# Four graph layers on one core: a new written order of steps, with buffers, first loads and both ends set anew

## The chip, the cores and the metric

The kernel runs on one NeuronCore of a Trainium2 chip. The metric is the device time of one execution in microseconds. Five engines work side by side, each through its own list of instructions in order: TensorE (PE, with weight loads shown as PEld), VectorE (DVE), ScalarE (ACT), GpSimd (POOL) and SyncE (SP), which here issues nearly all DMAs. A DMA that has to wait for its data holds up every DMA behind it in the same engine's queue.

## The reference, cut to what matters

There are 64 independent graphs, each with 256 nodes of 256 features (`x`) and a 256 x 256 adjacency (`adj`). Four layers follow each other, and each one adds its result to its input and normalizes the rows.

```python
x = layernorm(x + L0(x, adj))  # 4-head masked attention, output projection Wo, norm
x = layernorm(x + L1(x, adj))  # norm, 8-head masked attention on itself, MLP 256-1024-256 with gelu
x = layernorm(x + L2(x, adj))  # softmax of leaky_relu(s1_i + s2_j) over the mask, times x W
x = layernorm(x + L3(x, adj))  # softmax of leaky_relu(x diag(a_k) x^T) over the mask, times x
```

Everything is float32. For adjacencies of zeros and ones only, `L3` uses `a0` alone.

## The kernel before, in words

`usual_input` does all the work for adjacencies of zeros and ones that are the same both ways; a second path, `any_input`, follows for other inputs and isn't entered here. A flag that is worked out at the end decides.

One graph goes through seven Python generators, called threads, and every `yield` ends a step. A graph has 93 steps:

- `a` (19 steps, a0 to a18): a0 loads adj, a1 turns it to bf16 on ScalarE (`adjb`), a2 transposes it by DMA (`adjT`), a3 loads x twice, once as it is (`x0`) and once in blocks (`turned`). Then come the mask (VectorE), xT (a VectorE transpose of `turned`), x + beta, the projections q, k and v with their copies out of PSUM, the score products, two exponentials times mask, their sums `ea`, and the value product with the softmax sums.
- `u` (11): u0 inverts the sums on VectorE (`few`, `back`), u1 stores them to DRAM (`lines`), u2 loads them back spread over the partitions (`rr`), u3 multiplies; then the product with Wo, statistics, residual, norm (`z`, `xb`).
- `z` (4): stores z to DRAM (`rows`), loads it back in blocks (`blk`, four DMAs), turns the blocks on VectorE (`t`), scales them.
- `b` (8): second attention. `w` (9): its output goes through DRAM (w0 store, w1 load, w2 turn), statistics (w3), then the MLP's input does (w6 store, w7 load, w8 turn).
- `c` (8): first MLP product and gelu, four times. `o` (34): second MLP product, then layers 2 and 3; two more trips through DRAM, named n2 (o5 store, o6 load, o7 turn) and n3 (o18, o19, o20); o33 stores the result.

A transpose of a 256 x 256 tile is thus, in most places, a store of two DMAs, a load of four and one VectorE instruction. For the first and last graphs `DIRECT` names transposes that TensorE does instead; the first graph's x is one of them.

The order of all steps of all graphs is written out. `PLACES` gives each of the 93 steps a time in units of one graph's period; step i of graph g stands at g plus that time, and sorting gives one list. The list repeats with a period of 93 slots. `FIRST` and `LAST` are written lists of step names that replace its beginning (about the first seven graphs' worth) and its end (about nine). The wrapper `InOrder` keeps each engine's instructions in the order of this list; its line, 474, is therefore the line that nearly all instructions carry in the profile, so that they are told apart by their tiles. A wait comes from the data: an instruction waits until what it reads has been written, and until the last reader of the buffer that it writes is done. `BUFS` gives the number of buffers of each kind of tile.

`load_x(0)` and the loads of the first weights stand ahead of the list; further weights come in `l` steps on SP's queue, and `p` steps prepare constants.

Of the kernel before, what the change touches and what calls it, by code (L numbers as in the profile page):

```python
# [8 lines left out]
F32 = mybir.dt.float32  # L9
BF16 = mybir.dt.bfloat16  # L10
I32 = mybir.dt.int32
U8 = mybir.dt.uint8
AF = mybir.ActivationFunctionType
ALU = mybir.AluOpType
AX = mybir.AxisListType

P = 128
N = 256
D = 256
NC = D // P  # L20
G = 2
QB = N // P
# [19 lines left out]
SQ = True  # L42
XQ = True
DIRECT = {0: ('x', 'z', 'o'), 63: ('yT', 'n2', 'n3', 'o')}
BUFS = {'t': 5, 'q': 3, 'k': 2, 'v': 4, 'y': 4, 'z': 4, 'xb': 4, 'both': 3, 'xn': 6, 'mask': 8, 'e': 6, 'x0': 4, 'turned': 2, 'blk': 3, 'oT': 2, 'zs': 1, 'rr': 2, 'xT': 2, 'qT': 2, 'kT': 2, 'adj': 2, 'adjb': 2, 'adjT': 2, 'hT': 2}
PLACES = {
# [11 lines left out]
}  # L58
FIRST = (
    "a0a1l0a0a0a0a0a0a2a1a1a0a0a0a0a0a0a0a0a0a1a0a0a0a1a1a1a1a2a0u0a1a1l0a1p0a3a4a2u0a2a2a2a3a2a1a1a1a2u0u0u0a1a1"  # L60
    "a1u0a4a5a3l0a2a2a2u0a2a3l0a3a3u0u0a1a2a1u1a4a3a2a2a2a2u1u1a3a3a4a3a3a3a6u0u0a3a3u1a4a4a3a3a2a2z0a5z0a4a6l0l0"
    "u1u2l0a3u2u2z0z0a3p0u1u1a3u3u3u1a5b0b0a4u2b0b0p0u3a5b0u2u2b0a4a4a5u1a4a4a4u2u3a4a5u2a4l0a6u1z1a7a4u2b0b0u3u3"
    "w0w0a4a4w0a4u2z1z1u4a5a5w0u3a5a5z1p0a6a6u4a6a6p0w0u3a7p0z2z2z2u4a5w0u4a5a6a6a5a6a6w0w0u3b1b1b1b1b1b1w0u4u4z2"
    "b2b1c0p0u4u3z3z3b2b2b1b2c0c0b2z3w1w1u1a7w1c0c0c0c0c0w1o0w1b2o0o0o0z3b3b3b3u4b2a7w1b3b3b2b3a6w1a5a5a5a5w1w1w2"
    "o0o0w2a6a6b3a5b3a6o0a5a6u5u5c1c1c1c1c1a7c1c1a6a6w3a7c1u5a7a7u2w2w3o0u4a6a7u5u4w2w2z4u5u5w2u5a8a9u6u6z4u6o0w2"
    "u3w3u5z4o1o1u5w3w3w2a7u6z4b4o1o1o0o0o0a7b4w2u6b4b4u5b4o1u6w3z5a7a7w3z5b4w3c2c2z5o0z5a7o0o0o0o0u6c2c2c2c2c2u6"
    "c2o2o1o1o1o0o2u6o0o0u4a7a7b5a8a9b4o0o0o2a7a8a7b5b5w3b4a7b5o2o0b5b5u5o0o2a9w4u6w4w4w4w4o2o2c3c3c3c3c3c3c3c3o0"
    "o1o1z6b5o2b5o0o0o0o0o0o0z6z6o0o2a8a9o3o1o2o2u7o0z6w5o1o3aau7w4w4a8a8u7o3o3b6o2b6o1o1o1o1b6b6o3b6w5aau7b6w4o1"
    "w4a8a8a8a8a8a8o2o0o2o2o2a8a8o1a8a8w5c4c4o3a8w5c4c4c4o3c4c4c4o2u7u7u7o2o4w5o1o1o2o4o2o1o1w5aau7u7o1o1o4u7z7o3"
    "b6b6o2o2a8o4o1w6w5a8o1o1o1o1o1o1o1o2o2a9w5a9u8u8o3o3a9aba9w5a9a9a9a9a9a9o1o4u6o2o2u7o3w6o2w6w6o3o2o2c5a9a9c5"  # L70
    "u8u8abc5c5z7z7o3o3o3o3z7acc5a9aac5u8o4u8o4abo3o3o3o3c5c5u8o4a9aaaau8aab7aau8a9aaw6w6u9u9u9o4o4o3o2o2u8aao5o2"
    "b7b7z8b7o2aao4o4b7o5o1")
LAST = (
    "b7o5aaadw6o2o3o3u9o5aaw6u9z8o3aao5b7z8u9u9aaaaaao5z8b8o5u9o5b7b8b8aaaab8u9c6c6o4uao4c6o3c6o4o4c6w7w7w7o4u9c6"
    "c6c6o3o6o6uaz9w7w7w7uao3uaz9uaz9w7w7abo6o5b8b8uauaw7z9b9b9b8b9o5b8b9o5o5w8c7o4o4o4c7uao3o3uaabacababc7c7c7c7"
    "o5o5u8u9o6o3o3c7uac7abababo3w8w8abo4aco5o5acw8w8b9ababb9o3o7abzazao4o4o7o6w8o6w8ababo6abado5o7o4b9zazab9w9o7"
    "o7o4w8ababubo7o6acw9acbao4o4o4o4o5o4w8baado5aeo7o4o6o6acacacacbao4acacw9acbao5w9babaubo4ubo6o6w9c8c8c8afo5ub"
    "c8o7c8c8c8c8acacubaco3o4ubo6o6o5o5o5w9aco5adw9ado7o7adadacacucububaebabao7o7w9w9adadadadadadadubo5ucwao7ucuc"
    "o7o5o5adado6o5ubzbc9c9adafo7uco6o6o7uco7ucadado6o5o5o5o7c9udo8c9uawawawac9wac9zbududzbudzbucc9c9uco6o7ubbbo6"
    "o6bbo7o7o8o8uducududo8udzcbbzcaeo6wawabbo7o6o7o6o7o6o7zcbbaeo8udbbzco9o9o9udwawabco9bcbcbbbbaeaeaebczdzdbcbc"  # L80
    "cacacacacacacao5wbwbwbzdcawboaoaoaoazdbdbdwbbdbcbcbdo5afo6o7wbo6o6o7o8o8o6o7o7afafo9o6o6o7o7bdbdaeo6oawcwco7"
    "aeaeafafaeaeo6o9oawbwbbdbdo7o8ucwcaewcwco9oaaeaeaewbaewdwdo8o8wcwcudo9afafafafafafafafafaeafaeueueuewcoaafo8"
    "afo8o9oao9oawdwdcbcbo9oacbcbcbcbufueo9oawdo8o8ufo6o7o8wdo8o9o9oaoao9oao9oao8wco8wdo9ueueueueoacccccccccco9uf"
    "cbueccoaufwdcbwdo8o8o8ufufufufo8ueueobzeobufufzecczezezfcdcdobobo9ccbebebeo8o8oboazfzfo9ocoabebebeobococufzf"
    "cdo8bfbfbfcdbebebfcdcdocwecdcdo9oabfbfo8o8o9obobocododo8ododo8oao9weo9o8weodo8oaoaweobobocodo9oaocodbfbfo9oa"
    "o9oao9oaweweo9oaweocodweo9oao8o9oaobobo8ococodo9oaweobobobobodcecececececewfwfcecewfo8wfwfobocodo9o9obwfocod"
    "oeoeoeocococwfwfocoaoeoeobobodoaodododocwfcfcfodcfcfcfocoboboecfcfcfofofoeodoeoeocoeoeodofofofobocodococofoe"
    "odoeoeoeoeobofofodoeofofoboboboeobobofofobocobobofofofocofofobododoeoeococococococofofoeoeoeocofofofodododod"
    "odoeoeocofofododoeofoeoeoeoeoeodocofofoeofofofofofobocodoeodoeofof")
AHEAD = 16  # L90


# [356 lines left out]
def usual_input(ctx: ExitStack, tc: tile.TileContext, a: dict, out: bass.AP, flag: bass.AP):  # L449
# [62 lines left out]
    def load_edges(g):  # L512
        adj = new(io, [P, TB, N], I32, "adj")
        SP.dma_start(adj, a["adj"][g].rearrange("(q p) k -> p q k", p=P))
        return adj

    def load_x(g):
        turned = None
        if FX and "x" not in DIRECT.get(g, ()):
            turned = new(io, [P, NC, N // 32, 32], F32, "turned")  # L520
            parts = a["x"][g].rearrange("(t i) (c k j) -> k i c t j", i=32, c=NC, j=32)
            for k in range(P // 32):
                if XQ:
                    SP.dma_start(turned[32 * k:32 * k + 32], parts[k])
                for c in range(0 if XQ else NC):
                    SP.dma_start(turned[32 * k:32 * k + 32, c], parts[k, :, c])
        x0 = new(io, [P, TB, D], F32, "x0")
        SP.dma_start(x0, a["x"][g].rearrange("(q p) d -> p q d", p=P))
        return x0, turned
# [22 lines left out]
    def load_column(src, n, name, queue=None):  # L552

        t = const.tile([P, n // P], F32, name=name)
        load(queue, t, src.rearrange("(c p) -> p c", p=P))
        return t
# [3 lines left out]
    def load_all(src, name, at=None, queue=None):  # L560
# [2 lines left out]
        load(queue, t, src.unsqueeze(0).to_broadcast([P, D]))  # L563
        return t

    x_first = load_x(0)
    first = load_edges(0), x_first
    wqT = load_rows("L0_gnn_WqT", D, ACT)
    wkT = load_rows("L0_gnn_WkT", D, ACT)
    bq = load_column(a["L0_gnn_bq"], D, "bq", ACT)  # L570
    bk = load_column(a["L0_gnn_bk"], D, "bk", ACT)
    wvT = load_rows("L0_gnn_WvT", D, ACT)
    beta0 = load_all(a["L0_gnn_beta"], "beta0", queue=ACT)
    later.append([])
# [137 lines left out]
    def thread_a(g, s):  # L712
# [3 lines left out]
        ACT.activation(adjb, adj, AF.Copy, accum_out=there[:, g:g + 1])  # L716
        ACT.activation(adj.bitcast(F32), adj, AF.Square, bias=minus_half, accum_out=edges[:, g:g + 1])
        yield
        pt = new(io, [P, QB, N], BF16, "adjT")
        for q in range(QB):  # L720
            SP.dma_start_transpose(pt[:, :, q * P:(q + 1) * P], adjb[:, q, :])
        yield
        x, turned = first[1] if g == 0 else load_x(g)
        s["x"] = x
        yield
        mask = s["mask"] = new(act, [P, QB * N], BF16, "mask")
        DVE.scalar_tensor_tensor(mask, pt.rearrange("p k q -> p (k q)"), 1.0, adjb.rearrange("p t k -> p (t k)"),
                                 ALU.mult, ALU.min, accum_out=both_ways[:, g:g + 1])
        yield
        xT = new(act, [P, NC, N], F32, "xT")  # L730
        if FX and "x" not in DIRECT.get(g, ()):
            DVE.transpose(xT.rearrange("p c t -> p (c t)"), turned.rearrange("p c t j -> p (c t j)"))
        else:
            pt = new(ps_m, [P, NC, N], F32, "pm", 4)
            for t in range(TB):
                for c in range(NC):
                    transpose(pt[:, c, t * P:(t + 1) * P], x[:, t, c * P:(c + 1) * P], ident)
            ACT.copy(xT, pt)
        yield
        DVE.tensor_tensor(x, x, over_blocks(beta0), ALU.add)  # L740
        yield
# [30 lines left out]
        for c in range(NC):  # L772
            es.append(exp_of(ps[c], 64 ** -0.5, mask, None, c, 0))
            yield
        ea = [new(act, [P, 2, N], F32, "ea", 2) for _ in range(NC)]
        for c in range(NC):
            DVE.tensor_tensor(ea[c], es[c][:, :, 0:N], es[c][:, :, N:2 * N], ALU.add)
        yield
# [424 lines left out]
```

## Time and profile before

| | |
|---|---|
| median of 3 runs | 2404.54 us (2403.76 to 2405.94) |
| the profiled execution, its own time | 2405.76 us |
| its span, first to last instruction | 2404.0 us |
| busy: PE, DVE, ACT, POOL | 2351.7, 1924.6, 1827.0, 739.3 us |
| DMA | 265.61 MB, mean 110 GB/s; SP's queue busy 50.8% of 16 engines' span |
| SP's longest waits | for ScalarE's `xn` 245.2 us, `z` 114.7, `xb` 112.6; for the landing of `rows` (from xn) 103.8, of `lines` 87.0 |
| VectorE's longest wait | for the landing of `blk`, 295.5 us in 114 times |

Idle time of an engine costs something only where the engine, or one that waits for it, sets the end. Matmuls overlap, so a mean of 379 ns for one product of 256 columns is its time from start to end, not the distance to the next one.

### The profile page before, as it was taken

The page shows a single profiled execution, that of the slowest core. Times are in us where ns is not written, and L with a number is a line of the kernel's source. Part 1 is how long each engine was busy: PE and PEld are TensorE (multiplying, and loading weights), DVE is VectorE, ACT ScalarE, POOL GpSimd, SP SyncE. Part 2 cuts the span into 40 slices and gives each one's busy share as a digit, 9 for nine tenths or more (in the row PEclk, how much of TensorE's full clock was granted, in tenths as well). Part 3 has the DMA queues.
Part 4 walks back from the last instruction along what each step waited for, and adds up shares of the span by engine and source line. Part 5 has one row for each costly group of instructions (what it writes and reads, how often), then busy time and mean ns, then how long its engine had stood idle before and what let it go on. Part 6 is the DMA issues. An engine that isn't in the chain of part 4 may idle for free.

```text
span 2404.0 us, 49948 instructions
## 1 busy us (share of the span) xinstructions
PE 2351.7 (98%) x16116; PEld 1873.4 (78%) x16116; DVE 1924.6 (80%) x6175; ACT 1827.0 (76%) x3975; POOL 739.3 (31%) x1740
## 2 busy tenths in 40 slices
PE   7899999999999999999999999999999999999997
PEld 5677777877878777778778788787787788777776
DVE  5888778788787787887887888877878888888764
ACT  5777777777777877778777778778778778777666
POOL 1222233333323333323233233233333333323222
PEclk9999999999999999999999999999999999999999
DMA  6555545555554554545555555555555555445432
GB/s 149 107 107 102 120 106 110 110 117 111 109 119 104 114 119 105 117 107 112 117 113 109 120 112 110 121 108 112 122 106 116 121 108 115 106 108 108 93 77 72
DMA packets 1092021, 265.61 MB, mean 110 GB/s; under 512 B 861988, under 2 KB 1091368, under 8 KB 1091752
## 3 DMA queue, kind: packets, MB, share of 16 engines
q1 hardware_dynamic: 1090248, 261.42, 50.8%
q8 instruction: 130, 2.13, 0.4%
q14 instruction: 139, 1.14, 0.2%
q10 hardware_dynamic: 1504, 0.92, 0.1%
HBM read 153.63 MB, written 100.14 MB: 106 GB/s over the span
## 4 chain that ended last, share of the span: by engine, by line
PE 41%; DVE 24%; DMA 13%; SPq 8%; ACT 6%; POOL 5%; issue 3%; DVEq 0%; ACTq 0%; POOLq 0%
PE pm L474 36%; SPq L474 8%; DMA blk<-rows 7%; DVE e L474 6%; DVE y L474 4%; PE ps L474 4%; DVE t L474 3%; DMA lines<-back 3%; POOL nm L474 2%; ACT e L474 2%; DVE st L474 2%; POOL rstd L474 2%; DVE q L474 2%; ACT xb L474 1%; DMA turned<-in_x 1%
## 5 line engine op out<-in xcount | busy, mean ns | idle before, releaser
L474 PE MATMUL pm<-t,L_gnn_W 128*128 128x256 f32 x2048 | 471.2, 379 | 1.1 <-DVE t L474 1.0
L474 PE MATMUL pm<-L_gnn_W,hT 128*128 128x256 f32 (+1 forms) x2064 | 462.5, 379 | 0.0
L474 DVE STREAM_TRANSPOSE t<-blk 128x512 f32<-128x512 f32 x314 | 214.0, 693 | 295.5 <-DMA blk<-rows 295.5
L474 PEld LDWEIGHTS pm<-t,L_gnn_W 128*128 128x128 f32 x2048 | 388.0, 190 | 56.5 <-issue 2.1
L474 PEld LDWEIGHTS pm<-L_gnn_W,hT 128*128 128x128 f32 (+1 forms) x2064 | 384.9, 189 | 51.5 <-issue 0.7
L474 ACT ACTIVATE e<-ps 128x1024 f32<-128x1024 f32 x384 | 380.4, 1014 | 43.3 <-PE ps L474 42.3
L474 DVE SCALAR_TENSOR_TENSOR e<-e,mask 128x256 f32<-128x256 f32 x1024 | 369.9, 419 | 39.2 <-ACT e L474 39.1
L474 POOL TENSOR_SCALAR ve<-mv 128x2 f32<-128x2 f32 x192 | 70.3, 366 | 1061.7 <-DVE mv L474 1033.7
L474 POOL TENSOR_TENSOR rstd<-ve,mhalf 128x2 f32<-128x2 f32 (+1 forms) x384 | 340.4, 886 | 32.0
L474 ACT ACTIVATE hT<-pm,b 128x256 f32<-128x256 f32 x512 | 206.3, 470 | 21.2 <-PE pm L474 18.7
L474 POOL TENSOR_SCALAR ve<-sq 128x2 f32<-128x2 f32 x256 | 67.1, 262 | 496.3 <-ACT xn L474 407.5
L474 ACT ACTIVATE xn<-y,sums 128x256 f32<-128x256 f32 x256 | 127.5, 499 | 59.3 <-DVE y L474 58.6
L474 ACT ACT_TABLE_LOAD x127 | 162.9, 1283 | 8.4 <-DMA L_gnn_WkT<-in_L_gnn_WkT 6.8
L474 DVE TENSOR_TENSOR e<-e,mask 128x1024 f32<-128x1024 f32 x128 | 150.7, 1218 | 15.6 <-ACT e L474 15.2
L474 PE MATMUL ps<-t 32*128 32x256 f32 x2048 | 150.2, 400 | 2.3 <-ACT e L474 2.0
L474 ACT ACTIVATE xn<-y,nm,rstd 128x256 f32<-128x256 f32 x256 | 139.3, 595 | 12.2 <-POOL nm L474 7.4
L474 ACT ACTIVATE xb<-y,nm,rstd 128x256 f32<-128x256 f32 x128 | 69.8, 592 | 100.0 <-POOL v L474 91.0
L474 PE MATMUL pm<-v,q 128*128 128x260 f32 x512 | 139.4, 399 | 2.7 <-DVE q L474 2.3
L474 POOL TENSOR_SCALAR nm<-nm 128x2 f32<-128x2 f32 x320 | 132.0, 413 | 28.0
L474 PEld LDWEIGHTS ps<-t 32*128 32x128 f32 x2048 | 95.1, 184 | 53.1 <-issue 43.7
L474 PE MATMUL pm<-e,v 128*32 128x256 f32 x2048 | 123.4, 381 | 12.1 <-ACT oT L474 9.7
L474 PE MATMUL pm<-xT,L_gnn_WqT 128*128 128x256 f32 x512 | 125.0, 388 | 7.0 <-ACT xT L474 4.5
(144 smaller groups left out, 4611.7 us busy)
## 6 DMA issues: line engine op xcount, KB each, us to landing
blk<-rows SPq DMA_DIRECT2D x1256, 64.0 KB, 2.4
rows<-xn SPq DMA_DIRECT2D x252, 128.0 KB, 1.9
x<-in_x SPq DMA_DIRECT2D x64, 256.0 KB, 3.3
adj<-in_adj SPq DMA_DIRECT2D x64, 256.0 KB, 3.1
rr<-lines SPq DMA_DIRECT2D x128, 128.0 KB, 3.7
out<-xn SPq DMA_DIRECT2D x64, 256.0 KB, 3.3
turned<-in_x SPq DMA_DIRECT2D x252, 64.0 KB, 2.6
rows<-z SPq DMA_DIRECT2D x126, 128.0 KB, 1.9
```

The lines of the kernel that those rows point to most:

```text
L474: ins = call(*args, **kw)
```

## The change

The list of places is new throughout, and with it `FIRST` and `LAST`. `BUFS` shares memory out in another way: more `t`, `mask`, `e`, `blk`, `oT` and `ea`, fewer `k`, `v`, `both`, `x0`, `xT`, `qT`, `kT`, `adjb` and `adjT`. Wq and Wk are loaded on SP's queue between x and adj, and the biases bq and bk on GpSimd's queue; ScalarE begins with a small exponential. The first graph's xT is copied out of PSUM by VectorE instead of ScalarE. In thread `a` the mask and xT change places. The instructions are otherwise the same.

```diff
-BUFS = {'t': 5, 'q': 3, 'k': 2, 'v': 4, 'y': 4, 'z': 4, 'xb': 4, 'both': 3, 'xn': 6, 'mask': 8, 'e': 6, 'x0': 4, 'turned': 2, 'blk': 3, 'oT': 2, 'zs': 1, 'rr': 2, 'xT': 2, 'qT': 2, 'kT': 2, 'adj': 2, 'adjb': 2, 'adjT': 2, 'hT': 2}
+BUFS = {'t': 7, 'q': 3, 'k': 1, 'v': 3, 'y': 4, 'z': 4, 'xb': 4, 'both': 2, 'xn': 6, 'mask': 9, 'e': 7, 'x0': 3, 'turned': 2, 'blk': 4, 'oT': 3, 'zs': 1, 'rr': 2, 'xT': 1, 'qT': 1, 'kT': 1, 'adj': 2, 'adjb': 1, 'adjT': 1, 'hT': 2, 'ea': 3}
 PLACES = {
-    "a": (0.00000, 1.05376, 1.37634, 1.75269, 1.91398, 2.02150, 2.23656, 2.27957, 2.35484, 2.43011, 2.44086,
-        2.61290, 2.64516, 2.66667, 2.70968, 2.72043, 2.84946, 2.93548, 3.01075,),
-    "u": (3.06452, 3.21505, 3.22581, 3.68817, 3.78495, 3.87097, 3.92473, 4.07527, 4.33333, 4.48387, 5.24731,),
-    "z": (4.52688, 4.69893, 4.76344, 4.82796,),
-    "b": (4.94624, 5.10753, 5.45161, 5.53763, 5.58064, 5.63441, 5.88172, 5.95699,),
-    "w": (6.11828, 6.19355, 6.30107, 6.40860, 6.50538, 6.51613, 6.59140, 6.73118, 6.74193,),
-    "c": (7.15054, 7.16129, 7.20430, 7.26882, 7.29032, 7.32258, 7.38710, 7.41936,),
-    "o": (7.49462, 7.56989, 7.60215, 7.65591, 7.86022, 7.96774, 7.98925, 8.12903, 8.46237, 8.47312, 8.54839,
-        8.55914, 8.67742, 8.80645, 8.81720, 8.89247, 8.97850, 9.13978, 9.18280, 9.34409, 9.36559, 9.62366,
-        9.77419, 9.79570, 9.90323, 10.03226, 10.04301, 10.08602, 10.09677, 10.17204, 10.25807, 10.31183,
-        10.39785, 10.83871,),
+    "a": (0.00000, 0.37634, 0.79570, 0.87097, 1.19355, 1.19356, 1.32258, 1.33333, 1.45161, 1.51613, 1.54839,
+        1.58065, 1.62366, 1.65591, 1.73118, 1.75269, 1.90323, 1.97849, 2.03226,),
+    "u": (2.05376, 2.06452, 2.18280, 2.44086, 2.69893, 2.78495, 3.02150, 3.09677, 3.13978, 3.34409, 3.55914,),
+    "z": (3.39785, 3.47312, 3.56989, 3.77419,),
+    "b": (3.88172, 3.92473, 3.93548, 4.01075, 4.26882, 4.48387, 4.89247, 4.98925,),
+    "w": (5.22581, 5.66667, 6.16129, 6.24731, 6.35484, 6.40860, 6.49462, 6.74193, 6.80645,),
+    "c": (7.04301, 7.07527, 7.12903, 7.17204, 7.20430, 7.21505, 7.23656, 7.25807,),
+    "o": (7.27957, 7.31183, 7.38710, 7.52688, 7.86022, 7.95699, 8.15054, 8.29032, 8.43011, 8.50538, 8.68817,
+        8.72043, 8.82796, 8.83871, 8.84946, 8.91398, 8.96774, 9.08602, 9.11828, 9.53763, 9.60215, 9.64516,
+        9.76344, 9.81720, 9.94624, 10.36559, 10.41935, 10.46237, 10.59140, 10.63441, 10.67742, 10.70968,
+        11.30108, 11.61290,),
 }
...
+    ACT.activation(few_out[:, 0:1], minus_half, AF.Exp)
     x_first = load_x(0)
+    wqT = load_rows("L0_gnn_WqT", D, SP)
+    wkT = load_rows("L0_gnn_WkT", D, SP)
     first = load_edges(0), x_first
-    wqT = load_rows("L0_gnn_WqT", D, ACT)
-    wkT = load_rows("L0_gnn_WkT", D, ACT)
-    bq = load_column(a["L0_gnn_bq"], D, "bq", ACT)
-    bk = load_column(a["L0_gnn_bk"], D, "bk", ACT)
+    bq = load_column(a["L0_gnn_bq"], D, "bq", POOL)
+    bk = load_column(a["L0_gnn_bk"], D, "bk", POOL)
...
-        yield
-        mask = s["mask"] = new(act, [P, QB * N], BF16, "mask")
-        DVE.scalar_tensor_tensor(mask, pt.rearrange("p k q -> p (k q)"), 1.0, adjb.rearrange("p t k -> p (t k)"),
-                                 ALU.mult, ALU.min, accum_out=both_ways[:, g:g + 1])
...
-            ACT.copy(xT, pt)
+            DVE.tensor_copy(xT, pt)
+        yield
+        mask = s["mask"] = new(act, [P, QB * N], BF16, "mask")
+        DVE.scalar_tensor_tensor(mask, edgesT.rearrange("p k q -> p (k q)"), 1.0, adjb.rearrange("p t k -> p (t k)"),
+                                 ALU.mult, ALU.min, accum_out=both_ways[:, g:g + 1])
...
-        ea = [new(act, [P, 2, N], F32, "ea", 2) for _ in range(NC)]
+        ea = [new(act, [P, 2, N], F32, "ea") for _ in range(NC)]
```

The strings of `FIRST` and `LAST`, which are replaced as a whole, are left out here. The new `FIRST` covers 643 steps of the list (644 before) beside those of `l` and `p`, and `LAST` covers 843 in both. In the new `FIRST`, two of the first nine entries are loads of further weights that stand before the first graph's mask, and one stands ahead of everything else.

More of the change, by code (lines that the diff above doesn't have):

```diff
@@ L46 @@
 PLACES = {
[11 rows of a table removed]
[11 rows of a table added]
 }
 FIRST = (
[L60 to L69, printed above, removed]
@@ L70 @@
-    "b6b6o2o2a8o4o1w6w5a8o1o1o1o1o1o1o1o2o2a9w5a9u8u8o3o3a9aba9w5a9a9a9a9a9a9o1o4u6o2o2u7o3w6o2w6w6o3o2o2c5a9a9c5"
-    "u8u8abc5c5z7z7o3o3o3o3z7acc5a9aac5u8o4u8o4abo3o3o3o3c5c5u8o4a9aaaau8aab7aau8a9aaw6w6u9u9u9o4o4o3o2o2u8aao5o2"
-    "b7b7z8b7o2aao4o4b7o5o1")
-LAST = (
[L74 to L89, printed above, removed]
@@ new lines @@
+    "l0a0a1a0a0a0a0a2l0l0a0a0a0a0a0a0a0a1a1a1a0a0p0a0a0a0a0a0u0a1a1u0u0u0a2a1a1a1a1a3a1a1a1a1a1l0u0a1a1a2a2a2a2a1"
+    "u0a3a1u1u1a3u0u0a2a2u1a2a2a2a2a3u0a2a2a2a2u0a2a2u1l0z0a2a3u1z0u2a4a3a3u2z0z0u2u1b0a4a4p0u1u0u1b0b0a4u1u2a3a3"
+    "a3a3b0b0b0u1z1a5a3a3a4a3a3a3z1a4u2b0b0l0u2a5a3a3w0l0z1z1a3u3w0w0u2w0u2p0a6a4a4p0p0w0a4a4a4a4u2a4a4a4a4b1w0a4"
+    "a4a5a5a5a5a5b1b1a4w0u2w0l0b1b1b1u3u3a5a5a5a5a5a5a5b1u4u4u4w0c0p0p0a6a5a5b1c0c0c0c0c0c0c0a7u3u4a5a5u1u3w1a6a5"
+    "w1w1u5w1z2z2z2z2w1u3u4u4o0w1u3u5u5u4u3u4u5w1w1b2o0a8w1o0b2b2b2u3u4u5u5o0a6b2a6u3u4z3u5u2c1z4u5c1o0a6a6c1c1c1"
@@ new lines @@
+    "c1c1c1o1z3z4z3z4b2u3o1o1u4o0o0o0z3u5a7b3b3b3z4b2b3b3b3o0b2w2a7a7w2o0b4o1b3b4b4b4b4b3w3o0b4a6a6a6a6o0u5a6a7a6"
+    "a6a7a7a7o0a6z5w2a6a9z5a7a8a8a8o1a7o0a7a6o0o1w2o0a7a7a6w2o0z5w2a6u6b4b4w2a7u5z5a8a8a8a8a7a7a7b5a7u6a8o1o1o1o0"
+    "b5a7u7w3w2w2a8a8w3w3w3o1c2c2c2o0a8a8u6u6w4o1o1c2u7u6o0o0w3u7u6u6c2c2c2c2u7w3o1o1o1o1w4o0u7u7o0b5o1u7o0w3w3a9"
+    "u6u7o1o1b5u6b5b5o2o2o2o1w4u7a9c3c3u6u7z6z6o1a8o1a9w4o2c3c3c3c3o2z7c3c3o3o3a8a8o2b5z6w4o3o3z6a8a8w4w4o0a9a9a9"
+    "b5w5a8b6o0o0o0a9aau8w4b6o0a9a9b6u6u8b6o1aab6b6o0o2o2a9a9o3o0w5u8w4o1a9a9a9a9a9o3o2o2z7z7z7w5w5b6a9a9b6b7u9u7"
@@ new lines @@
+    "o0abo3o3o2o2u9u9c4c4c4c4o3w5w5w5w5u8o3o1aao2o2o2c4o2u9b7u8b7c4u8o0c4b7w5u8u8c4o2b7aaaao2o2o3acu9o4o3o4u9o4u8"
+    "o2o1o3u8z8w6o3b7w6o1o1o1o1o1o1aaaaaaz8o2o2aaaaaaaao2aao2u9u9aaz8o3o4b7aao3aaaaaaabb7z8b8o3aau9abb8o3b8abo4c5"
+    "c5uao4c5b8uao0o3u8o2")
+LAST = (
+    "o1c5c5c5c5c5o5w6w6o5ababb8u9uauao4o5adb8w6acabo3o3o5abw7w7w7abababababababababo3o4o4acw6w6o5o5w6b8b8w8ababo2"
+    "o2w7o5uaubuao4o4o3o3o3c6o5ubc6o2o2o2c6c6c6c6uac6o2uao2aec6w7o4uaububw7w8o4o4o2z9z9aco5uao1u9uao4w8o4o5z9z9o6"
+    "o6aczazao6w8w7o4o5o5zao6ububb9b9b9o4acaco6w7aco2acb9o5o6zaaco5o5b9b9acacaco5w8acacaco3o3aco3o5o3w7o6o6bab9ub"
+    "b9w9w9acacuco3o3w8w8o6babaw8w8o6c7o3c7c7c7c7c7c7c7o5uco4o4adubububucuco7o7uco7o7ubuco5o4o7bauco6o4o4o6w9w9o5"
+    "o5o4c8c8c8adadc8o3o3c8c8c8uco6o7ado5o5c8uczbadw9o5o5afw9uco6o6o6o6o8w9w9o8o8babao6o4o5o4o5adadzbzbo7adadadw9"
+    "adadadadadbazbbbzcbaadadbbbbbbo4o5ado7o7o4wao6aeo5zcudo4zcbbbbo7c9o4o5c9c9o5o4o5aeaeaeaeaeo8o6udc9c9c9o6udc9"
+    "o7o7aezco6udc9aeaeaeo8wawawaaeaeaeaeaeudududaeafafafbco4o5bbudaebcbcaebbueuewbbco9wawao7udo7afo7o7o7o9o9o9wa"
+    "udbco6bcwbueo6o6ueafafafafafo7ucafafafafafwawaafbco6bco6o9o6o6o6zdzdo6wbuewbo6caueuecao8o9wbo7o7o7wbcacacaca"
+    "wbcacaafo4o5wbzdueuezdo8o8oaoaoao7o6o9wbbdwcbdo9bdafafuebdzeo6bdwcbdzeo8o9o8o9o7o8o9ufufo7oaoaufo8o9wccbcbcb"
+    "cbcbcbcbzezewcwccbufbebdbdo7o7o7o8o9o8oao9o8o8o7o9oao9bewcwco8o8o9ufufo9ufwdoboboawcwco7ufbeo7oaufo8o9o8o9be"
+    "oao7wdobo8o7ufudo7o7o8oboaoazfzfccccccobo9ccwdwdccccccccocwdwdwdoazfoaoaoaocbeoczfbebfbewdwdcdobbeweweoaocue"
+    "weufcdocobcdcdweoacdweo8oaoacdcdcdodo9o9o8ococobo8weo9o9oaododbfbfbfo8o8o9o9o8o8o9o9o8o9o8bfoaoco8o9bfobobo9"
+    "oaoaococo8weweweodbfbfobocceceodobocwfwfwfoacececeoboco9cececeobododoaocwfwfobocobocoawfoaoaoaoaoaodobocoao8"
+    "oewfwfwfobobococoeoeoecfcfcfcfoeoboccfcfcfobocoeoeodcfofodododobocofoeo9oeoeoaofofododododoeoeobofocodoeobob"
+    "oeoeocodoeofofodoeobodobobocofofobobofobofofoeocococobocododococofofofodofofodobododofododoeoeoeoeodofofofof"
+    "oeofoeoeocofododoeoeofodoboeoeoeocofofofoeoeofofofofodoeofocodoeof")
@@ L718, in thread_a @@
         yield
-        pt = new(io, [P, QB, N], BF16, "adjT")
+        edgesT = new(io, [P, QB, N], BF16, "adjT")
         for q in range(QB):
-            SP.dma_start_transpose(pt[:, :, q * P:(q + 1) * P], adjb[:, q, :])
+            SP.dma_start_transpose(edgesT[:, :, q * P:(q + 1) * P], adjb[:, q, :])
         yield
```

## The prediction

> **What bounds the kernel now.** First the page's row of engine totals: TensorE is busy for all but 52 us of the span. The Trainium skill (Perfetto Trace Analysis, Identifying the Most-Contended Engine) warns that matmul busy time is a poor measure of headroom, and weight loads here fill 78% only, so I don't rest on that row. I read the chain of waits next, to see whether TensorE really sets the pace.
>
> ```profile
> PE 2351.7 (98%) x16116; PEld 1873.4 (78%) x16116; DVE 1924.6 (80%) x6175; ACT 1827.0 (76%) x3975; POOL 739.3 (31%) x1740
> ```
>
> The chain has two forms. From about 1335 to 1965 us it is TensorE alone, and repeats exactly:
>
> ```profile
> 1374.87 17.56 PE pm L474 x81
> ...
> 1411.06 17.57 PE pm L474 x81
> ```
>
> That is 36.19 us for a graph, the price of its 252 matmuls. Before that, from about 430 us on, it goes round through SP's queue and the transfers:
>
> ```profile
> 682.69 2.39 DMA lines<-back
> ...
> 685.10 0.63 SPq L474
> ...
> 688.12 3.83 DMA blk<-rows
> ...
> 692.08 0.71 DVE t L474
> ...
> 696.45 1.08 ACT xb L474 x2
> ```
>
> Read downwards: SP stands still until the little store `lines` has landed, issues two `rr` and four `blk` loads, VectorE waits for the blocks, then come statistics, GpSimd, ScalarE, and SP again. The chain's list has `lines<-back` at 682.69 and, 17 graphs later, at 1308.46: 36.81 us each, 0.62 more than TensorE needs. The table by stretches (columns: us, then busy time and instructions of PE, PEld, DVE, ACT, POOL, the clock, DMA share, GB/s) says the same, and shows both ends:
>
> ```profile
> 0.00:60.00 60.00, 47.61 (x340) 35.20 (x344) 32.06 (x66) 33.15 (x75) 6.37 (x17) 1.00 0.63 149
> 60.00:120.00 60.00, 53.15 (x400) 39.45 (x393) 51.97 (x193) 45.37 (x85) 15.38 (x29) 0.97 0.54 108
> ...
> 430.00:1335.00 905.00, 895.56 (x6166) 712.97 (x6164) 732.88 (x2354) 697.78 (x1517) 292.24 (x662) 1.00 0.52 112
> 1335.00:1965.00 630.00, 629.77 (x4375) 506.18 (x4376) 523.52 (x1679) 497.74 (x1087) 207.33 (x471) 1.00 0.53 114
> ...
> 2340.00:2404.00 64.00, 51.22 (x242) 42.74 (x240) 31.28 (x103) 42.11 (x111) 19.26 (x65) 0.93 0.29 72
> ```
>
> TensorE is idle 12.4 + 6.9 us in the first 120 us, 3.6 us from 120 to 430, 9.4 us from 430 to 1335, 0.2 us from 1335 to 1965, and 20 us after (6.9 from 2100 to 2340, 12.8 from 2340 on). Idle alone understates the loop: 6166 matmuls at the later rate (4375 in 630 us, 6.944 per us) need 888 us, so 17 us went there. The period gives 0.62 x 24.6 graphs = 15 us; I take 15.
>
> **What the skill says.** DMA: Bandwidth & Descriptors (Anatomy of one DMA) puts a fixed cost of about 2.0 us on a DMA, mostly until its write is confirmed, and says that a wait is served by the issuing sequencer. The trace agrees: `lines` is 16 KB and lands in 2.0 us by median, `rows` in 1.9 to 2.9, `blk` in 2.4, and SP stands behind its own stores. Its Rules for kernel authors say to issue early and wait late; that is what slots decide here.
>
> **The change: places.** Each graph makes 93 steps; every engine runs its instructions in the written order. One slot is 36.2/93 = 0.39 us. What a leg needs: a store and its landing (0.4 to 1 us of issue, then 2 to 2.9) 6 to 10 slots; a four-part load (four issues of 0.49 us, then 2.4) 11, and 15 with the 3.83 us seen in the chain. Slots given, before to after:
> - `lines` store to `rr` load (u1 to u2): 1 to 11. SP's stall of 87 us in the run, on `lines`, should go; `rr` to its use falls from 43 to 24, still 9 us for a landing of 3.7.
> - store to block load: z 16 to 7, attention output 7 to 41, MLP input 13 to 23, n2 2 to 18, n3 15 to 39. Only z gets less, and 7 slots (2.7 us) are about one store.
> - block load to VectorE's turn: 6 to 9, 10 to 46, 1 to 6, 13 to 13, 2 to 6. Three stay shorter than 11, so VectorE will still wait, some 2 us each. It is busy 80%, and TensorE reads the turned blocks 13 or more slots later (z 29, MLP input 22, n2 13, n3 15), which hides that.
> - statistics to scaling, where GpSimd takes about 2 us: w3 to w5 10 to 15, n3's 31 to 32 8 to 55.
>
> No arithmetic is added or taken away, so TensorE's 36.2 us stay. All that can be won in the middle is the loop's 15 us. The loop misses by 0.62 us of a period, under two slots, and `lines` alone gives back up to ten; I credit 14 to 16, value **15**. What is late next: TensorE itself. The nearest new handover on it is the q projection's PSUM tile, drained by ScalarE one slot before n3's value product wants it. Between a7 and that product lie 1.7 us (o8) of TensorE work against 0.84 us of draining, so about nothing; but its bound is 0.5 us a graph over 48 graphs, 24 us, which goes into the range. The second is the MLP: its last gelu is now two slots before its first reader (seven before). At the end of the run a second product starts at 2356.33 while its gelus run until 2358.43, so the wait is by parts; 0 to 0.2 us a graph.
>
> **Buffers.** xT, qT, kT, adjb, adjT and k go to one, v, x0 and both lose one; t, mask, e, blk, oT and ea gain. In the new places each is released before the next graph asks: adjb is held 0.82 of one period (17 slots spare), both 1.51 of two, x0 2.23 of three; mask was held 7.99 of eight and now 8.75 of nine. Zero, covered by those spare slots; if they are eaten, ScalarE's conversion of the next adjacency waits, which TensorE sees through the mask, some 76 slots on. Masks are made behind xT instead of ahead of it: 0.69 us of VectorE, swapped, zero.
>
> **First loads and first x.** The timeline of the start:
>
> ```profile
> 4.68 1.08 PE L474 MATMUL pm<-ident,x 128*128 128x128 f32 x4 [4.68 <-DMA x<-in_x]
> ...
> 6.78 1.28 ACT L474 ACT_TABLE_LOAD   x1 [6.78 <-DMA L_gnn_WkT<-in_L_gnn_WkT]
> ...
> 9.62 0.56 ACT L474 COPY xT<-pm 128x512 f32<-128x512 f32 x1
> 10.23 3.78 PE L474 MATMUL pm<-xT,L_gnn_WqT 128*128 128x256 f32 x8 [4.47 <-ACT xT L474]
> ```
>
> The first copy sits on ScalarE behind six DMA issues, a table load and two passes over adj. On VectorE, idle until 12.69, it starts when the transposes end, 5.8, and takes 0.56: projections from 6.4, if Wq is there. Wq is issued second on SP, at 1.2, and landed in 4.1 on ScalarE's queue; two more loads beside it make that 5.3 to 6.5. Gain 10.2 - 6.4 = **3.8 us**; bounds 1.5 and 4.5. The early Exp moves the 1.28 us table load to where ScalarE has nothing (ScalarE: Activation LUTs, What ACT_TABLE_LOAD costs, has 1283 ns; the trace's mean is 1283 too). adj goes past two loads of 0.5 us issue, and adjb starts near 6.7 instead of 8.08. bq and bk leave ScalarE's queue for GpSimd's, which no row here shows: the same page on DMA (Latency and other measured facts) has about 1 us against 0.6 to the first byte. They are wanted after the first projection, 10.2; bk took 6.2 us before, so nothing to +3 us, value nothing. The projections' first 8 matmuls take 3.78 us, later ones 1.99; TensorE: Matmul & The Clock Gate (Part 1) explains slow first microseconds, and they stay.
>
> The new opening order: apart from the 4.7 + 4.5 us already told, TensorE idles about 13.6 us until 430, for oT, xT and e, all behind transfers. More room there might take all of it, or a deeper pipeline (11.6 periods against 10.8) cost 4: I take **-4**, from +4 to -12.
>
> **New ends.** 20 us are idle after 2100; the last 8 us (values, moments, GpSimd, store of 3.3) can't go. Of the other 12 I take a third, **-4**, from +5 to -10.
>
> **Sum.** 15 + 3.8 + 4 + 4 = 26.8 us off the profiled execution's 2405.76 us (span 2404.0, 1.8 around it): 2379. That execution lies 1.2 us over the median, so against the median 2404.54 - 26.8 = **2378 us**. A floor: 64 x 36.2 = 2317 us of products, 4.7 until the first x, 8 to drain, some 20 for a pipeline that can't be full at its ends: about 2350.
>
> **Rivals.**
> 1. The loop closes again at another place. For: three block loads still have 6 to 9 slots, and VectorE waits 295.5 us for blocks now, 5 us a graph even in the TensorE-bound stretch. Against: that same stretch. If half of the graphs run at 36.8, 0.6 x 24 = 15 us come back: no gain in the middle, **2393**.
> 2. Slower: VectorE's crowded slots from 84 to 5 of the next period (ea, two masked exponentials, n3's masking, statistics, sums turned: 8.6 us by their rows in 14 slots, 5.4 us) set a longer loop, since lines' values are made right there and SP waits one slot later for them. The 48 graphs in the written middle took 25 x 36.81 + 23 x 36.2 = 1753 us; with 12 us from the ends it decides at (1753 + 12)/48 = 36.77 us a graph. At 37.2 it is 1786: 33 - 12 = 21 us more, **2425**. Against: VectorE is idle a fifth of each period and should catch up.
> 3. The places do what they say, but the opening and end lose what the middle wins: +9 instead of -12, **2399**.
>
> **How the numbers follow.** Main case 0.72 (its own range 2362 to 2390), rival 1 0.14, rival 3 0.06, rival 2 0.08. A difference under 0.2%, 4.8 us, can't be told from none here. The range takes main case, rival 1 and part of rival 3: 2360 to 2397. Faster: 0.72, 0.13 of rival 1, 0.02 of rival 3: 0.87. Same 0.05, slower 0.08.
>
> **What would show it.** Right: the chain from about 400 us on is TensorE alone at 36.2 us; SP's wait for `lines` far under 87 us; TensorE's first projection near 6.4 us; TensorE idle under 2 us from 430 to 1965. Wrong: SP or `blk` in the middle of the chain, a period over 36.5, or repeated TensorE waits for ScalarE at the value product or gelu.

## The result, and the profile after

The changed kernel takes 2374.86 us (median of 4 runs, 2371.1 to 2378.5), against 2405.24 us for the kernel before beside it. The ratio is 0.9871, with a 95% interval of 0.9848 to 0.9894: some 30 us or 1.3% less. The prediction was 2378 us. The profiled execution has a span of 2375.9 us, 28.1 less than the 2404.0 of before.

First the same row of the page, engine totals:

```profile
PE 2337.0 (98%) x16116; PEld 1880.2 (79%) x16116; DVE 1924.6 (81%) x6176; ACT 1822.8 (77%) x3977; POOL 686.2 (29%) x1742
```

The share of TensorE is 98% as before, and says nothing. The table by stretches, with the columns of before (us, busy time and instructions of PE, PEld, DVE, ACT, POOL, clock, DMA share, GB/s), says where the time came from:

```profile
0.00:60.00 60.00, 48.33 (x324) 34.56 (x328) 31.42 (x75) 30.04 (x67) 8.39 (x21) 0.94 0.55 124
60.00:120.00 60.00, 56.58 (x462) 40.60 (x454) 53.18 (x167) 42.91 (x84) 13.33 (x27) 1.00 0.54 122
430.00:1335.00 905.00, 905.00 (x6320) 733.04 (x6309) 751.53 (x2419) 709.52 (x1553) 272.19 (x681) 1.00 0.54 115
1335.00:1965.00 630.00, 630.00 (x4349) 511.67 (x4349) 521.57 (x1672) 497.49 (x1090) 188.08 (x470) 1.00 0.53 114
```

From 430 to 1965 us TensorE has no hole at all; 6320 matmuls now fit where 6166 stood. The first minute is hardly better. And the chain of waits, in the stretch of 682 to 757 us in which SP, `lines` and `blk` stood before (start, us, what):

```profile
684.27 22.79 PE pm L474 x105
707.06 1.93 PE ps L474 x16
708.99 5.16 PE pm L474 x26
...
720.32 22.79 PE pm L474 x105
```

It is TensorE alone, and repeats after 36.05 us (36.04 on average). That is less than the 36.19 us that TensorE needed for a graph before, when it was alone on the chain too.

To add this up I charge each matmul its mean distance from start to start in TensorE's own stretch of the kernel before (1340 to 1966 us), by kind. What a stretch takes beyond that sum is lost. (The few kinds that don't occur there are charged by an estimate that shifts both columns alike by a us or two, so only the differences count.)

| stretch | lost before | lost after |
|---|---|---|
| 0 to 430 us | 33.5 us | 31.0 us |
| 430 to 1960 us | 15.4 us | -6.4 us |
| 1960 us to the end | 26.0 us | 22.3 us |

The middle gives 21.8 of the 28.1 us: 15.4 for the loop, 6.4 because TensorE's products themselves became cheaper. Opening and end give 2.5 and 3.7 in this pair of executions, and single executions of the changed kernel lie up to 7 us apart, so those two are not firm.

### The profile page after: what moved, and what is told of

It reads as the page before. It is cut to its first block, busy times and chain, and to the rows that moved or that the text cites. A ratio compares the mean times of both kernels' runs of the same rounds, so it can differ in the third digit from the quotient of the medians.

```text
span 2375.9 us, 50126 instructions
## 1 busy us (share of the span) xinstructions
PE 2337.0 (98%) x16116; PEld 1880.2 (79%) x16116; DVE 1924.6 (81%) x6176; ACT 1822.8 (77%) x3977; POOL 686.2 (29%) x1742
## 4 chain that ended last, share of the span: by engine, by line
PE 87%; DVE 4%; ACT 3%; DMA 2%; SPq 1%; POOL 1%; issue 1%; DVEq 0%; POOLq 0%; ACTq 0%
PE pm L474 77%; PE ps L474 10%; SPq L474 1%; DVE e L474 1%; DVE y L474 1%; DMA blk<-rows 1%; ACT e L474 1%; POOL rstd L474 0%; ACT xn L474 0%; DMA rows<-z 0%; DVE t L474 0%; DVE st L474 0%; DVE q L474 0%; ACT z L474 0%; DMA adj<-in_adj 0%
## 5 line engine op out<-in xcount | busy, mean ns | idle before, releaser
L474 PE MATMUL pm<-t,L_gnn_W 128*128 128x256 f32 x2048 | 461.0, 382 | 0.4 <-DVE t L474 0.4
L474 PE MATMUL pm<-L_gnn_W,hT 128*128 128x256 f32 (+1 forms) x2064 | 455.2, 379 | 0.2 <-PE ps L474 0.2
L474 POOL TENSOR_TENSOR rstd<-ve,mhalf 128x2 f32<-128x2 f32 (+1 forms) x384 | 316.7, 825 | 32.0
L474 POOL TENSOR_SCALAR ve<-sq 128x2 f32<-128x2 f32 x256 | 74.3, 290 | 771.0 <-ACT xn L474 533.0
L474 POOL TENSOR_SCALAR ve<-mv 128x2 f32<-128x2 f32 x192 | 49.3, 257 | 810.9 <-DVE rz L474 454.8
L474 DVE STREAM_TRANSPOSE t<-blk 128x512 f32<-128x512 f32 x314 | 221.0, 705 | 37.8 <-DMA blk<-rows 36.7
L474 ACT ACTIVATE hT<-pm,b 128x256 f32<-128x256 f32 x512 | 201.5, 474 | 18.2 <-PE pm L474 17.5
L474 ACT ACTIVATE few_out<-few 128x8 f32<-128x8 f32 x64 | 13.3, 208 | 165.0 <-DVE few L474 164.9
L474 DVE SCALAR_TENSOR_TENSOR y<-pm,r,xn 128x256 f32<-128x256 f32 x256 | 123.9, 484 | 9.9
L474 PE MATMUL pm<-xn,q 128*128 128x257 f32 x512 | 130.5, 381 | 1.4 <-ACT q L474 1.4
```

The source lines that it names most:

```text
L474: ins = call(*args, **kw)
```

## The experiments

Groups of runs ran on different chips, each beside the kernel before, whose median lay between 2398.45 and 2405.24 us; ratios are to that one. In the five kernels that move a place, the written middle is put together anew: `FIRST` and `LAST` stay, and every step that they don't hold comes in between, sorted by its place. That alone changes nothing: in rr_later, the first below, the traces show the same order on all five engines as in the kernel before.

**Which link of the loop?** The prediction had put most weight on SP's stand behind `lines`. Two kernels open one link each in the kernel before.

```diff
 # rr_later
-    "u": (3.06452, 3.21505, 3.22581, 3.68817, ...
+    "u": (3.06452, 3.21505, 3.33333, 3.68817, ...
 # turn_later
-        ... 9.34409, 9.36559, 9.62366,
+        ... 9.34409, 9.47312, 9.62366,
```

> The kernel before with one place changed: the rr load (u2) stands 11 slots after the lines store (u1) instead of 1. Theory A (the loop hangs on SP standing still for lines): SP's wait for lines falls from 87 to under 30 us, the chain is TensorE alone at 36.2 us a graph from about 430 us on, and the time falls by 10 to 15 us, to 2389 to 2395. Rival B (the loop hangs on the block loads that have 1 or 2 slots until their turn): the period stays at 36.6 or more and under 4 us are won. Rival C (one loop with several short links, slack in any of them opens it): as A.

> The kernel before with one place changed: the turn of n3 (o20) stands 12 slots after its block load (o19) instead of 2; the rr load stays 1 slot after the lines store. Theory A: SP still stands still for lines, about 87 us, the period stays at 36.6 or more, under 4 us are won. Rival B and rival C: the chain becomes TensorE alone at 36.2 us, 10 to 15 us are won.

rr_later: 2399.07 us, ratio 0.9997 (0.9987 to 1.0007). turn_later: 2382.35 us, ratio 0.9934 (0.9918 to 0.9951), or 16.6 us less by the medians, the whole loop. Only VectorE's order differs there. Theory A expected the opposite. In turn_later the chain is TensorE alone:

```profile
701.18 17.57 PE pm L474 x81
...
737.38 17.56 PE pm L474 x81
```

That is 36.20 us, the old price of the products, although SP waits for `lines` as long as ever (waits of SP's queue: us in total, times, longest):

```profile
SPq L474 <- DMA lines<-back: 82.8, 56, 4.2
```

So SP's stand costs nothing where the turn has room. But rr_later hadn't touched it, so it tests nothing: SP has no other instruction between slots 21 and 31, so its list is the same in both orders, and with 85.0 us its wait is too. The next kernel moves the `rr` load behind SP's next instruction instead.

```diff
 # rr_behind
-    "u": (3.06452, 3.21505, 3.22581, 3.68817, ...
+    "u": (3.06452, 3.21505, 3.34946, 3.68817, ...
```

> The kernel before with the rr load (u2) moved behind the block load of n3 (o19) on SP's queue. In the earlier try nothing of SP's stood between its old and its new place, so SP's order, and with it the program, was the same. Now SP issues the n3 load without standing still for lines first. Rival C (one loop with several short links, and SP's stall is one of them): the n3 blocks land 2 to 4 us earlier, the chain becomes TensorE alone at 36.2 us, 10 to 16 us are won. Rival B (only the two slots between the n3 load and its turn count): under 4 us are won.

2384.06 us, ratio 0.9939 (0.9922 to 0.9955), or 15.4 us less. Only SP's order differs. Its wait for `lines` falls to 13.8 us, and the chain is TensorE alone here as well:

```profile
SPq L474 <- DMA lines<-back: 13.8, 9, 4.1
...
701.28 17.57 PE pm L474 x81
...
737.48 17.56 PE pm L474 x81
```

So rival C holds: one loop, SP's stand, n3's block load and its turn, VectorE, GpSimd, ScalarE and SP again. Making room at either of two of its links opens it, and neither link alone is "the" cause. Both kernels keep the old buffers, so the loop's 15 us need none of the new ones. The other direction, in the changed kernel:

```diff
 # rr_at_once
-    "u": (2.05376, 2.06452, 2.18280, 2.44086, ...
+    "u": (2.05376, 2.06452, 2.07527, 2.44086, ...
```

> The changed kernel with one place put back: the rr load 1 slot after the lines store instead of 11. Theory A: SP's wait for lines returns, above 80 us, and with it the loop: a period of 36.4 to 36.8 us and 15 to 35 us more than the changed kernel (2390 to 2410). Rival C (the other links now have slack enough): SP's wait returns but the period stays at 36.04 us and the time within 2 us of 2375.

SP waits for `lines` again, and nothing follows (first the changed kernel's wait, then this one's):

```profile
SPq L474 <- DMA lines<-back: 16.4, 10, 2.5
...
SPq L474 <- DMA lines<-back: 67.5, 57, 2.5
```

The period stays 36.04 us and the time 2371.81 us, ratio 0.9894 (0.9875 to 0.9913), which can't be told from the changed kernel's (0.9871 to 0.9887 in three groups on other chips). The room at the other legs is enough without the eleven slots.

**Where do TensorE's own 0.16 us a graph come from?** The order of the products is all that differs. Before, a graph goes from full 128 x 128 products to products on part of the array and back in three places (b3; a13; b6, a17 and b0 together); after, in two: b0, b6, a17 and b3 stand in one group, and only the scores (a13) stand apart. By the part of the array that a product uses (128x128, 64x128, 32x128 or 128x32 in the traces), the order changes kind seven times a graph before and six times after. One kernel pulls that group apart, which makes eight:

```diff
 # pe_apart
-        8.72043, 8.82796, 8.83871, 8.84946, 8.91398, ...
+        8.72043, 8.82796, 8.83871, 8.89785, 8.91398, ...
```

> The changed kernel with one product moved in the written middle: one half of layer 2's value product (o14) stands between the two value products on 32-column tiles (b6 and a17) instead of ahead of the group of row- and column-tiled products. Theory (TensorE's own period hangs on how often the order goes from full to tiled products and back): two more changes at about 0.1 us each, a period of 36.2 to 36.3 us instead of 36.04, still without a wait, and 8 to 12 us more than the changed kernel. Rival (the changes cost nothing, and 36.20 to 36.04 has another cause): the period stays within 0.05 us of 36.04.

2389.66 us, ratio 0.9963 (0.9949 to 0.9978); the changed kernel in the same group took 2372.25 us, ratio 0.9887 (0.9867 to 0.9906), so 17 us were added. No wait of TensorE appears in the middle, and the chain is TensorE alone at another period:

```profile
725.72 22.79 PE pm L474 x105
...
762.09 22.79 PE pm L474 x105
```

That is 36.37 us (36.38 on average), 0.33 more and above the theory's 36.2 to 36.3. From the starts of the matmuls: the step from one 32-column product to the next took 0.196 us, and now 0.309 and 0.313 us are paid around the intruder, which alone would take 0.22: 0.21 us for the two changes. Another 0.1 us lies inside the value product itself (mean distance 0.237 instead of 0.2195 us), as it did in the kernel before; what delays it there I can't tell. The Trainium skill (TensorEngine Tiling (Array Packing), Key Properties) says that changing the tiling mode drains TensorE. These runs show no drain as such, but agree that a change costs time, and give the price in this kernel: each of the changes that occur takes 0.304 to 0.313 us from start to start, where the next product or group of the same kind would come after 0.195 to 0.22. Leaving a group of 32-row products, for one, costs 0.304 us instead of 0.195.

That the order has a price is thus shown. Of the 0.16 us between before and after, the one change fewer makes up 0.10. The rest is the net of small delays inside runs of full products, in the same traces: 0.10 less in the value product and 0.06 less at one product with `ident`, but 0.10 more among the 32 products of `t` and a weight. Their cause stays open.

**Start and opening.** One kernel puts back the loads and the copy at the start:

```diff
 # old_start
-    ACT.activation(few_out[:, 0:1], minus_half, AF.Exp)
...
-    wqT = load_rows("L0_gnn_WqT", D, SP)
-    wkT = load_rows("L0_gnn_WkT", D, SP)
     first = load_edges(0), x_first
-    bq = load_column(a["L0_gnn_bq"], D, "bq", POOL)
-    bk = load_column(a["L0_gnn_bk"], D, "bk", POOL)
+    wqT = load_rows("L0_gnn_WqT", D, ACT)
+    wkT = load_rows("L0_gnn_WkT", D, ACT)
+    bq = load_column(a["L0_gnn_bq"], D, "bq", ACT)
+    bk = load_column(a["L0_gnn_bk"], D, "bk", ACT)
...
-            DVE.tensor_copy(xT, pt)
+            ACT.copy(xT, pt)
```

> The changed kernel with the old loads and copy at the start: Wq, Wk, bq and bk on ScalarE's queue, no early exponential, first xT copied by ScalarE. Theory: the first projection begins near 10 us instead of 5.5, all of it is passed on, and the time is 3 to 5 us over the changed kernel (2378 to 2380). Rival: the changed kernel's opening waits for adj and its mask anyway (adj takes 6.6 us to land there), so the time is within 1.5 us of 2375, or less.

2375.48 us, ratio 0.9899 (0.9882 to 0.9915), against 0.9894 for rr_at_once, which equals the changed kernel in all but that stand, on the same chip. The first projection does begin at 10.20 us, but the difference of 3.7 us in the medians is inside both intervals: inconclusive as to time. In the one profiled execution of each, the second graph's first projection begins at 27.98 us here and at 24.87 us in rr_at_once, against 25.62 us in the kernel before. So the new order of the opening by itself seems to put it later, and the new loads bring it back.

The timeline of the changed kernel shows where its lead goes:

```profile
4.76 0.69 DVE L474 COPY xT<-pm 128x512 f32<-128x512 f32 x1 [4.76 <-PE pm L474]
...
5.50 3.78 PE L474 MATMUL pm<-xT,L_gnn_WqT 128*128 128x256 f32 x8 [0.78 <-DVE xT L474]
...
8.93 0.63 ACT L474 ACTIVATE adjb<-adj 128x512 bf16<-128x512 int32 x1 [6.69 <-DMA adj<-in_adj]
...
14.30 0.63 ACT L474 ACTIVATE adjb<-adj 128x512 bf16<-128x512 int32 x1 [1.94 <-DVE mask L474]
...
24.57 3.75 PE L474 MATMUL pm<-xT,L_gnn_WqT 128*128 128x256 f32 x8 [3.03 <-DVE xT L474]
```

The first projection is 4.7 us earlier than before. But adj, issued behind Wq and Wk and after Wv and beta on ScalarE's queue, needs 6.6 us to land, and the first adjacency is converted 0.85 us later than before. The second waits for the first mask, since there is one `adjb` now; behind it on SP's queue stand its transposes and the second graph's x, so that TensorE has nothing to do before 24.57 us. In the kernel before, the same projection of the second graph began at 25.62 us, so that about 1 us of the lead is left:

```profile
25.62 1.99 PE L474 MATMUL pm<-xT,L_gnn_WqT 128*128 128x256 f32 x8 [0.61 <-DVE xT L474]
```

It also ran faster there, in 1.99 us instead of 3.75. From 15 to 25 us TensorE is idle for 1.6 us before and for 5.4 us after, and behind that the granted clock (the number after the five engines) is 0.50. In adj_third, the first of the kernels below, it is idle for 3.5 us, and the clock stays at 1.00. The stretch of 25 to 30 us in the kernel before, the changed one and adj_third:

```profile
25.00:30.00 5.00, 4.39 (x22) 3.88 (x21) 2.09 (x6) 1.76 (x6) 0.00 (x0) 1.00 0.37 75
...
25.00:30.00 5.00, 5.00 (x13) 3.92 (x13) 0.01 (x1) 2.37 (x6) 0.00 (x0) 0.50 0.32 67
...
25.00:30.00 5.00, 5.00 (x32) 4.02 (x30) 0.35 (x1) 2.74 (x6) 0.00 (x0) 1.00 0.62 182
```

The clock is below 1.00 there in all five profiled executions with the changed opening and the changed first loads. What lowers it is not tried apart. Three kernels change the first loads further, with the changed kernel beside each group:

```diff
 # adj_third: all of these on SP's queue, in the order x, Wq, adj, Wk, Wv, beta
-    wkT = load_rows("L0_gnn_WkT", D, SP)
     first = load_edges(0), x_first
+    wkT = load_rows("L0_gnn_WkT", D, SP)
...
-    wvT = load_rows("L0_gnn_WvT", D, ACT)
-    beta0 = load_all(a["L0_gnn_beta"], "beta0", queue=ACT)
+    wvT = load_rows("L0_gnn_WvT", D, SP)
+    beta0 = load_all(a["L0_gnn_beta"], "beta0", queue=SP)
 # opening: also, in BUFS
-... 'adjb': 1, ...
+... 'adjb': 2, ...
 # opening2: also, in FIRST, its ninth and tenth entries moved
-    "l0a0a1a0a0a0a0a2l0l0a0a0a0a0a0a0a0a1a1a1a0 ...
+    "l0a0a1a0a0a0a0a2a0a0a0a0a0a0a0a1a1a1l0l0a0 ...
```

Expected of after_again:

> The changed kernel itself, beside the three others of this group on one chip: a period of 36.04 us and 1.0 to 1.4% under the kernel before.

Expected of adj_third:

> The changed kernel with another order of the first loads, all on SP's queue: x, Wq, adj, Wk, Wv, beta. Theory: adj lands near 6 us instead of 8.9, the first mask is done near 11 instead of 14.3, the first graph's exponentials and the second graph's adjacency follow, and 1 to 3 us are won against the changed kernel. Rival: one buffer of adjb and of adjT keeps the second graph waiting and TensorE's holes stay: within 1 us.

Expected of opening:

> As the run with adj third, and with two buffers for adjb. Theory: ScalarE no longer waits for the first mask before it converts the second graph's adjacency, the second graph's xT comes near 20 us instead of 24.3, TensorE's hole of 3.0 us before it closes, and 3 to 5 us are won against the changed kernel. Rival: holes move to later steps of the opening, and under 2 us are won.

Expected of after_third:

> The changed kernel beside the two others of this group: a period of 36.04 us, 1.0 to 1.4% under the kernel before.

Expected of opening2:

> The run with the new opening (adj third among the first loads, two buffers for adjb), and the second and third group of weight loads moved behind the second graph's x on SP's queue. Theory: that x starts 1 to 2 us earlier, TensorE's second hole shrinks by as much, and the kernel is 4 to 6 us under the changed kernel beside it. Rival: the weights are late for their first use, or the hole moves on: 2 to 4 us, as the new opening alone.

| kernel | median us | ratio (95% interval) | lost, 0 to 430 us |
|---|---|---|---|
| after_again | 2371.96 | 0.9882 (0.9865 to 0.9898) | 28.8 us |
| adj_third | 2371.57 | 0.9879 (0.9863 to 0.9896) | 25.5 us |
| opening | 2369.15 | 0.9876 (0.9860 to 0.9893) | 24.7 us |
| after_third | 2372.25 | 0.9887 (0.9867 to 0.9906) | 29.2 us |
| opening2 | 2371.69 | 0.9890 (0.9873 to 0.9907) | 26.8 us |

In the profiled executions the opening loses 2 to 4 us less in all three, and most of that comes with adj's place. With adj third, the second graph's first projection begins 1.3 us or more earlier than in any profiled execution with the changed opening (24.12 to 24.87 us). The second `adjb` adds nothing there (adj_third, then opening):

```profile
22.87 1.97 PE L474 MATMUL pm<-xT,L_gnn_WqT 128*128 128x256 f32 x8 [1.80 <-DVE xT L474]
...
23.13 1.96 PE L474 MATMUL pm<-xT,L_gnn_WqT 128*128 128x256 f32 x8 [1.81 <-DVE xT L474]
```

It does end a wait of ScalarE's in the first 45 us. In after_again that is

```profile
ACT adjb L474 <- DVE mask L474: 7.2, 3, 3.9
```

With adj third it is still 5.5 us, in `opening` the line is gone, and the opening's loss differs by 0.8 us between those two. In `opening2` the projection begins at 22.10 us, 1.0 earlier again, as its theory said. But the medians are only 0.4, 2.8 and 0.6 us below the changed kernel's beside them, where 1 to 3, 3 to 5 and 4 to 6 were expected, and the intervals overlap. None of the three is shown to beat the changed kernel.

## Why the prediction was right, point by point

- **The loop, 15 us**: measured 15.4 by the table of lost time, and 16.6 and 15.4 by turn_later and rr_behind. Its size came from two readings that needed no knowledge of the cause: the chain's period before, 36.81 us, and TensorE's own, 36.19.
- **What opens it**: SP's wait for `lines` fell as forecast, from 87.0 to 16.4 us, but the step failed that credited it with "up to ten" slots of relief as if SP's stand alone held the loop. Ten slots with nothing of SP's in between gave nothing (rr_later). Relief there is enough to open the loop (rr_behind), but not needed: more room at n3's turn opens it too, and in the changed kernel the `rr` load's place makes no difference. VectorE's wait for `blk`, expected to stay at some 2 us for each of three legs, fell from 295.5 to 36.7 us: the blocks mostly land before VectorE comes. Whether that is due to the slots, to the fourth `blk` or to VectorE coming later (it now waits 217.8 us for ScalarE's `e`, 54.4 before) was not tried apart.
- **What a leg needs**: the fixed cost of about 2.0 us that the prediction took from the Trainium skill (DMA: Bandwidth & Descriptors, Anatomy of one DMA) stands there for DMAs that GpSimd issues. `lines`, issued by SP, lands in 2.0 us by median before, which agrees, but in 1.4 us in the changed kernel.
- **TensorE's 36.2 us stay**: wrong. It was 36.04, and the term was missing from the sum: -6.4 us in the middle. No arithmetic changed, but the order of the kinds of products did, and the order has a price (pe_apart); 0.10 of the 0.16 us are accounted for by it.
- **Start, 3.8 us**: the first projection came 4.7 us earlier, of which 1.0 was x landing earlier (TensorE's first transpose at 3.64 instead of 4.68). The step on adj failed: adjb was expected near 6.7 us and came at 8.93, since only the issue was counted (two loads of 0.5 us) and not the bytes ahead of it. The loads ahead land first (Wk at 8.19, adj at 8.91 us), and with Wk, Wv and beta behind it adj lands at 7.08. The biases on GpSimd's queue landed at 7.43 and 9.08 us and were first wanted at 10.40: nothing, as taken.
- **The opening, -4 us**: wrong in sign in this pair. With the start's 4.7 us in it, the stretch to 430 us gained only 2.5, so the rest lost about 2. (Two more executions of the changed kernel, on other chips, lose 28.8 and 29.2 us there, so the rest would have gained nothing.) Some 3 us of what was lost before belong to the loop besides, which begins before 430 us: by the same sums, the stretch from 250 to 430 us loses 3.1 us in rr_later and 0.4 in turn_later, with the same opening. The forecast was a guess at idle time, with no reading of the new order. What it missed lies between 15 and 30 us, where 3.7 us were lost before and 9.2 after: adj's late landing, TensorE's longer idle, and the granted clock of 0.50 after it. "Zero, covered by those spare slots" for the single `adjb` fails as a reading, since the spare slots exist in the written middle only and ScalarE does wait in the opening; that this wait costs time is not shown.
- **The end, -4 us**: 3.7 in this pair, by executions that scatter by more than that. A guess that fitted, not a reading.
- **The handovers** on PSUM and at the gelu, bounded at 0.5 and 0.2 us a graph: no wait of TensorE between 430 and 1965 us, so nothing.
- **Rival 2**, VectorE's crowded slots: the wait it named is there, and is the longest of SP's in the middle (us in total, times, longest). The row names `y`, but the issue behind the wait is the `lines` store: in one graph SP is idle from 1005.8 to 1011.06 us, and `back`, which it stores, is done at 1011.03.

```profile
SPq L474 <- DVE y L474: 220.4, 45, 5.7
```

It is 5 us a graph and harmless: TensorE has no wait in that stretch. The total, 26.8 us against 28.1 in the profiled pair, came out close by luck: the missing 6.4 us, and an error of 5.3 us for start and opening together (7.8 forecast, 2.5 measured), have opposite signs.

## What to carry to other kernels

When the same written order runs through two stretches, one bound by a chain through queues and one by an engine, the difference of their periods is what relaxing the order can win, whatever the cause, as long as the new order leaves the engine's own period alone; here it was 15 us, and the engine's own period gave 6.4 more. Find the cause by opening one link at a time. A place in an order counts on one queue only by what stands before and after it there: moving a step past nothing changes nothing. Spare slots found in the repeating part say nothing of the opening, which has an order and waits of its own.

## What the runs showed of the hardware that was not expected

- An engine that is never idle can still get faster: the distances between TensorE's starts depend on the kind of the product before. The same 252 matmuls took 36.20, 36.04 and 36.38 us in three orders with seven, six and eight changes of kind, without a wait in any of them.
- The first loads land nearly in the order in which they are issued, whichever engine issues them, 256 KB some 0.7 to 0.8 us behind the load ahead. In the changed kernel Wk, adj and Wo, 256 KB each, were issued at 1.75, 2.27 and 2.78 us and landed at 8.19, 8.91 and 9.69. In adj_third adj was issued at 1.75 us, ahead of Wk, Wv and beta, and landed at 7.08, Wk at 7.80 and Wv at 8.55.
- The granted clock can fall in the middle of an opening: 0.50 from 25 to 30 us in the changed kernel, after 5.4 us of idle in the ten before, and 1.00 in adj_third after 3.5. The eight matmuls of one projection took 3.75 us and 1.97.
